# Four chained attention blocks on one core: the order of the first loads, of the first set-up instructions and of GpSimd's bias additions

## The chip, the cores and the metric

The kernel runs on one NeuronCore of a Trainium2 chip. The core has five engines that run side by side, each with an instruction queue of its own: TensorE (PE in the profile; PEld is its weight load), VectorE (DVE), ScalarE (ACT), GpSimd (POOL) and SyncE (SP). SP here only issues DMAs; ACT issues some too. 16 DMA engines carry the transfers of all queues. The metric is device microseconds (us) of one execution, and lower is better. Before the change it is 2193.79 us, the median of three runs (2191.36 to 2203.49).

## The reference

`x` is 8 batches x 256 tokens x 320 channels, all float32. Four layers follow each other, each working on the result of the one before:

```python
x = L0(x, ctx)   # self attention, cross attention, GEGLU; q, k, v and softmax weights rounded to 8 bits
x = L1(x, ctx)   # the same three steps without rounding
x = L2(x, ctx)   # two cross attentions (text and image tokens), sum, projection, residual
x = L3(x, ctx)   # cross attention with 8 heads plus a second attention over channels
```

The change touches L0 alone, whose two attentions are (20 heads of 16 channels):

```python
h = layer_norm(x);  q, k, v = fq(h @ Wq1), fq(h @ Wk1), fq(h @ Wv1)
x = softmax_q(q k^T / 4) v @ Wo1 + bo1 + x          # self
h = layer_norm(x);  q, k, v = fq(h @ Wq2), fq(ctx @ Wk2), fq(ctx @ Wv2)
x = softmax_q(q k^T / 4) v @ Wo2 + bo2 + x          # cross
```

`fq` divides by the largest magnitude in the whole tensor over 127, rounds, and multiplies back. `softmax_q` does the like with the softmax weights (over 255). So a step for all 8 batches has to end before any rounding can start.

## The kernel before

`x` stays in SBUF as `x_sb` (128 partitions, 16 token tiles, 320 channels). `Kernel.__init__` (L56) starts its load: `load_x` (L77) issues batch 0 on SP's queue and batches 1 to 7 on ACT's (L80). It then issues the loads of `cols` (gains, biases and small masks, one column each) on ACT's queue (L65, L67, L68; the second and third write rows that the first wrote too) and builds the identity matrices.

`open_flow` (L160) opens the pools and makes small masks on VectorE: `m32`, `half`, `magic` (L168 to L176). `open_quant` (L179) makes `place`, `rows`, `fill`, `sel` in the same manner (L184 to L202). None of these is needed by the first normalisation.

`load` (in `tile_xattn_kernel`, L1642) loads a layer's weights on SP's queue. `weight_q` (L233) is used for q and k of L0: 8 DMAs each, for each block of rows one of 256 channels (L242) and one of the last 64 channels, spread to 4 heads of 16 with gaps of 16 (L243, pieces of 64 bytes). `weight_v` (L263) makes 4 DMAs (L269), `weight_o` (L272) 5 (L276, L279), `load_ctx` (L82) 3 (L86).

The program is written with a scheduler that orders each engine's queue itself, from dependencies and its own estimates: what stands late in the text can be issued early. In the trace SP's queue has the 256-channel parts of q and k ahead of v, and the 64-byte parts of q and k only after a part of o and of ctx. GpSimd's bias additions, which stand late in the text (L1428), are issued soon after the last reader of their operand.

`Quant` (L1192) is one attention of L0; `s` is the self attention, `c` the cross one.

- `project_all` (L1218): for each batch, `normed` (L305) computes the mean and variance on VectorE (L314, L315, L317), the reciprocal root on GpSimd (L319), the normalised `xh` on VectorE (L322); `turned` (L327) transposes it on TensorE (L339) and ScalarE applies gain and bias (L347, four pieces, of which the last two take rows of `cols` in both halves); `duo`, `half_rows` and `whole_rows` (L122 to L139) multiply with v, q and k. The row blocks of 64 channels come first (L139), so that two of them run side by side on TensorE, and the next batch's transposes stand between them and the whole blocks (L132).
- `steps` (L1316) reduces the maxima to one scale each. `whole`, `whole_by_act`, `whole_v` (L1344, L1369, L1386) round q, k and v, mostly on GpSimd. `whole_all` (L1409) runs them all, and at its end adds the projection's bias row to `x`, one batch at a time, on GpSimd (L1428, 128 partitions x 640).
- `tops_all` (L1438) finds the row maxima (PE L1453, DVE L1456), splits them into three bf16 parts on VectorE (L1473, L1475), and `sums_all` (L1508) sums the exponentials (PE L1497 and L1519, ACT L1504). These two and `whole_all` are woven together.
- `weight_steps` (L1545) turns the sums into one scale (ACT L1549 and L1557, DVE L1552 to L1558); `shift` (L1561) makes each batch's offsets, nearly all on VectorE (L1565 to L1570).
- `out_all` (L1572) makes the weights (DVE L1606), multiplies with v (PE L1588), projects and adds to `x` (DVE L493), which needs the bias to be in it already. With the self attention's `out_all` run the cross attention's `queries_all` (L1288): `normed` again, with `xh` on GpSimd for six batches, and TensorE L120.

`behind` (L293) gives the scheduler an edge that puts one instruction after another on the same engine, without a semaphore. After L0 come L1 to L3 as a flow of `items`; the change does not touch them.

Of the kernel before, what the change touches and what calls it, by code (L numbers as in the profile page):

```python
# [11 lines left out]
F32 = mybir.dt.float32  # L12
BF16 = mybir.dt.bfloat16
AF = mybir.ActivationFunctionType
# [40 lines left out]
class Kernel:  # L55
    def __init__(self, ctx, tc, a, out):  # L56
        self.ctx, self.tc, self.nc, self.a, self.out = ctx, tc, tc.nc, a, out
        self.persist = ctx.enter_context(tc.tile_pool(name="persist", bufs=1))
        self.small = ctx.enter_context(tc.tile_pool(name="small", bufs=4))
        nc, pool = self.nc, self.persist  # L60

        self.x = pool.tile([P, NT, C], F32, name="x_sb")
        self.load_x(0, B)
        self.cols = pool.tile([P, NCOL], F32, name="cols_sb")
        nc.scalar.dma_start(self.cols, a["cols"])  # L65

        nc.scalar.dma_start(self.cols[64:, NCOL - H3 * T3 :], a["cols"][:64, NCOL - H3 * T3 :])  # L67
        nc.scalar.dma_start(self.cols[64:, 2:COL_B1:3], a["cols"][:64, 2:COL_B1:3])  # L68
        self.ident = pool.tile([P, P], F32, name="ident")
        make_identity(nc, self.ident)  # L70
        self.ident16 = pool.tile([P, P], BF16, name="ident16")
        nc.vector.tensor_copy(self.ident16, self.ident)
        self.nhalf = pool.tile([P, TPB], F32, name="nhalf")
        nc.gpsimd.memset(self.nhalf, -0.5)
        self.ctxT = pool.tile([P, 2, B, M], F32, name="ctxT")

    def load_x(self, b0, b1):  # L77
        xt = self.a["x"].rearrange("b (t p) c -> p (b t) c", p=P)
        for b in range(b0, b1):
            (self.nc.scalar if b else self.nc.sync).dma_start(self.x[:, TPB * b : TPB * (b + 1), :], xt[:, TPB * b : TPB * (b + 1), :])  # L80

# [78 lines left out]
    def open_flow(self, ctx):  # L160
        nc, tc = self.nc, self.tc
        self.ps_f = ctx.enter_context(tc.tile_pool(name="ps_f", bufs=3, space=PSUM))
# [3 lines left out]
        self.work = ctx.enter_context(tc.tile_pool(name="f_work", bufs=2))  # L166

        self.m32 = fk.tile([P, PAD], F32, name="m32")  # L168
        nc.vector.tensor_reduce(self.m32, self.ident.rearrange("p (j r) -> p r j", r=PAD), AX.X, ALU.add)
# [6 lines left out]
        nc.vector.tensor_scalar(self.magic[:, 2:4], self.half, -MAGIC, None, ALU.mult)  # L176
        self.count = 0

# [46 lines left out]
    def rows_of(self, w, src, filled=False):  # L225
# [5 lines left out]
        return [(w[:, 0], src[:P]), (w[:64, 1], src[P:])]  # L231

    def weight_q(self, tag, name, filled=False):  # L233


        n = -(-self.a[name].shape[0] // P)
        w = self.fw.tile([P, n, 3 * P], F32, tag=tag, name=tag)
        if n == 2 or filled:
            self.nc.gpsimd.memset(w[64:, 1] if n == 2 else w[:64, 2], 0.0)
        self.nc.gpsimd.memset(w[:, :, 2 * P :], 0.0)  # L240
        for dst, src in self.rows_of(w, self.a[name], filled):
            self.nc.sync.dma_start(dst[:, : 2 * P], src[:, : 2 * P])  # L242
            self.nc.sync.dma_start(  # L243
                dst[:, 2 * P :].rearrange("p (h r) -> p h r", r=PAD)[:, :, :D],
                src[:, 2 * P :].rearrange("p (h d) -> p h d", d=D),
            )
        return w
# [57 lines left out]
    def normed(self, b, ln, on=None):  # L305
# [15 lines left out]
        for t in range(TPB):  # L321
            (on or nc.vector).tensor_scalar(  # L322
                xh[:, t], x[:, t], mv[:, t, 0:1], rstd[:, t : t + 1], ALU.subtract, ALU.mult
            )
# [867 lines left out]
class Quant:  # L1192
# [25 lines left out]
    def project_all(self):  # L1218
# [8 lines left out]

        x = k.normed(0, self.ln)
        after = turn(0)
        for b in range(B):  # L1230
            xT = after
            if b + 1 < B:
                x = k.normed(b + 1, self.ln)
            q = self.q[b] = self.pool.tile([P, 3 * N], F32, tag="Q", name="Q", bufs=B)
# [151 lines left out]
    def whole_v(self, b):  # L1386
# [10 lines left out]
        for s in range(2):  # L1397
# [5 lines left out]
        yield  # L1403
        nc.gpsimd.tensor_scalar(
            vh[:ks, :kc, 16:, :D], tv[:ks, :kc, 2 * P :].rearrange("p t (h d) -> p t h d", d=D),
# [3 lines left out]
    def whole_all(self, b0=1):  # L1409
# [16 lines left out]
        for b in range(B):  # L1426
            x = k.x[:, TPB * b : TPB * (b + 1), :]
            k.nc.gpsimd.tensor_tensor(x, x, self.brow.unsqueeze(1).to_broadcast([P, TPB, C]), ALU.add)  # L1428
            yield
# [207 lines left out]
def kernel(ctx: ExitStack, tc: tile.TileContext, a, out):  # L1637
    k = Kernel(ctx, tc, a, out)
    with ExitStack() as es:
        k.open_flow(es)  # L1640

        def load(layer, q, kk, v, o, row):  # L1642
            plain = layer == "L0"
            w = {"q": k.weight_q("q", f"{layer}_xattn_{q}", q == "Wq2")}
            if kk is not None:
                w["k"] = (k.weight_q if plain else k.weight_k)("k", f"{layer}_xattn_{kk}")
                w["v"] = k.weight_v("v", f"{layer}_xattn_{v}")
            if o is not None:
# [6 lines left out]
        with tc.tile_pool(name="l0", bufs=1) as pool:  # L1655
            k.open_quant(pool)
            with tc.tile_pool(name="l0_keys", bufs=1, side="right") as kpool:
                s = Quant(k, pool, kpool, 0, *load("L0", "Wq1", "Wk1", "Wv1", "Wo1", 0), False)
                k.load_ctx()
                s.project_all()  # L1660
# [162 lines left out]
```

## Time and profile before

| what | value |
|---|---|
| runs | 2203.49, 2193.79, 2191.36 us |
| span of the profiled execution, first to last instruction | 2202.1 us |
| mean granted TensorE clock | 0.971 |
| TensorE busy | 2036.4 us, 92% |
| VectorE, ScalarE, GpSimd busy | 1112.6, 833.3, 330.5 us |
| first batch of `x` in SBUF (VectorE starts) | 4.51 us |
| ScalarE's table load | 15.90 us, 1.28 us long |
| last part of k's weights in SBUF (TensorE goes on) | 23.95 us |
| end of `project_all` on TensorE | 100.8 us |
| last instruction of `whole_v` on GpSimd, self / cross | 187.9 / 541.3 us |
| the 16 bias additions L1428 | first at 16.1, last at 396.2 us, 1.53 us shortest, 2.54 us longest |

The page of a profile gives the busy time of each engine, the busy tenths in 40 slices of the span, the chain of work that ended last, and groups of equal instructions with what ended the idle time before them. The trace can be asked further: the chain in order of time, the instructions of one engine in order of time (start, length, engine, line, operation, result<-operands, count), who waited for whom, and busy times by window. Only the span of the profiled execution is on the page; it lies 1.4 us under the slowest of the three runs.

### The profile page before, as it was taken

What the parts mean: (1) busy time and instruction counts of PE and PEld (TensorE: products, weight loads), DVE (VectorE), ACT (ScalarE), POOL (GpSimd) and SP (SyncE); (2) the same over time, 40 slices, a digit from 0 to 9 for tenths busy, and PEclk for the clock granted to TensorE, in tenths of its full rate; (3) what the DMA queues carried; (4) which work ended last, traced back from release to release, by engine and by line L of the source; (5) the groups of instructions that cost most, each with busy time, mean ns of one, the idle gap of its engine ahead of it and who ended that gap; (6) DMA issues with size and microseconds to landing.
All of it is one profiled execution on the core that took longest, in us unless ns stands there. A gap on an engine that the chain in (4) does not pass through costs nothing.

```text
span 2202.1 us, 38254 instructions
## 1 busy us (share of the span) xinstructions
PE 2036.4 (92%) x16415; PEld 1194.6 (54%) x16415; DVE 1112.6 (51%) x1698; ACT 833.3 (38%) x1259; POOL 330.5 (15%) x358
## 2 busy tenths in 40 slices
PE   7888889898889999999999998899999999999997
PEld 5643345554444465465555555544555655666664
DVE  5388687445651222235555567621121666546565
ACT  3456888367542121124444444311201333222221
POOL 3194033723010000000000010100000100000100
PEclk9989889898899999999999999999999999999999
DMA  4000000642120000020000101100000120000000
GB/s 118 20 12 2 2 1 1 174 111 57 52 85 14 1 0 1 1 93 2 2 2 22 28 25 36 47 1 0 1 0 1 24 68 23 19 16 26 23 19 16
DMA packets 79303, 63.21 MB, mean 29 GB/s; under 512 B 48410, under 2 KB 68318, under 8 KB 78622
## 3 DMA queue, kind: packets, MB, share of 16 engines
q1 hardware_dynamic: 75070, 57.06, 9.4%
q10 hardware_dynamic: 4064, 3.71, 0.6%
q8 instruction: 129, 2.11, 0.4%
q14 instruction: 40, 0.33, 0.0%
HBM read 42.61 MB, written 17.37 MB: 27 GB/s over the span
## 4 chain that ended last, share of the span: by engine, by line
PE 73%; DVE 15%; issue 4%; ACT 4%; POOL 2%; DMA 2%; SPq 0%; ACTq 0%; DVEq 0%; POOLq 0%
PE pf L594 13%; PE pf L120 11%; PE pf L132 9%; PE pa L120 7%; PE pa L456 6%; PE pf L439 4%; PE pa L594 3%; PE pf L139 3%; DVE negm L1456 3%; PE pf L394 3%; PE pf L736 3%; DVE rs L464 3%; PE pf L1497 2%; PE pa L1519 2%; DVE negm L401 2%
## 5 line engine op out<-in xcount | busy, mean ns | idle before, releaser
L445 ACT ACTIVATE e<-pf 128x1024 f32<-128x1024 f32 (+2 forms) x176 | 158.5, 946 | 220.1 <-PE pf L439 213.1
L401 DVE TENSOR_REDUCE negm<-pf 128x4 f32<-128x1024 f32 (+4 forms) x224 | 188.1, 887 | 97.9 <-PE pf L394 97.9
L594 PE MATMUL pf<-xTf,ff 128*128 128x512 f32 x512 | 230.8, 597 | 6.2 <-DVE negm L401 5.2
L464 DVE RECIPROCAL rs<-pa 128x256 f32<-128x256 f32 x88 | 152.3, 1745 | 143.5 <-PE pa L456 143.5
L1504 ACT ACTIVATE e<-pf,sc_s 128x1024 f32<-128x1024 f32 x160 | 169.8, 1118 | 48.7 <-PE pf L1497 44.8
L1456 DVE TENSOR_REDUCE negm<-pf 128x4 f32<-128x1024 f32 (+2 forms) x128 | 143.3, 1151 | 69.6 <-PE pf L1453 58.2
L619 DVE SCALAR_TENSOR_TENSOR hT<-pf,cols_sb,gl 128x512 f32<-128x512 f32 x64 | 48.0, 751 | 256.4 <-ACT gl L618 254.1
L120 PE MATMUL pf<-ff,hT 128*128 128x320 f32 x640 | 174.4, 434 | 0.0
L594 PEld LDWEIGHTS pf<-xTf,ff 128*128 128x128 f32 x512 | 94.3, 190 | 125.4 <-issue 118.5
L120 PEld LDWEIGHTS pf<-ff,hT 128*128 128x128 f32 x640 | 120.9, 190 | 55.5 <-issue 6.1
L618 ACT ACTIVATE gl<-pf,cols_sb 128x512 f32<-128x512 f32 x64 | 44.0, 689 | 247.8 <-PE pf L594 247.8
L439 PE MATMUL pf<-qT,kT 32*128 32x256 f32 (+1 forms) x1280 | 122.1, 410 | 9.1 <-DVE negm L401 7.5
L394 PE MATMUL pf<-kT,qT 32*128 32x120 f32 (+1 forms) x1920 | 113.1, 326 | 18.6 <-ACT e L445 18.3
L487 POOL TENSOR_TENSOR xb<-x_sb,brow 128x640 f32<-128x640 f32 x24 | 37.0, 1543 | 563.8 <-DVE x_sb L493 555.4
L120 PE MATMUL pa<-o,oT 128*128 128x320 f32 x352 | 105.7, 441 | 15.2 <-DVE oT L465 15.2
L394 PEld LDWEIGHTS pf<-kT,qT 32*128 32x128 f32 x1920 | 83.0, 186 | 58.4 <-ACT e L445 27.5
L647 POOL TENSOR_TENSOR xb<-x_sb,brow 128x640 f32<-128x640 f32 x16 | 25.0, 1563 | 573.8 <-DVE x_sb L652 528.2
L1497 PE MATMUL pf<-Q,K 32*128 32x256 bf16 (+1 forms) x960 | 90.5, 295 | 21.7 <-DVE negm L1456 11.5
L456 PE MATMUL pa<-e,v 128*32 128x256 f32 (+1 forms) x1280 | 106.1, 391 | 2.3 <-ACT e L445 1.7
L1606 DVE TENSOR_SCALAR w<-e 128x1024 bf16<-128x1024 f32 (+2 forms) x128 | 89.2, 703 | 32.3 <-ACT e L1504 31.1
L132 PE MATMUL pf<-xT,q 128*128 128x256 f32 x384 | 100.5, 391 | 0.4 <-ACT e L445 0.2
L439 PEld LDWEIGHTS pf<-qT,kT 32*128 32x128 f32 (+1 forms) x1280 | 68.4, 182 | 55.5 <-DVE negm L401 26.9
(291 smaller groups left out, 3439.2 us busy)
## 6 DMA issues: line engine op xcount, KB each, us to landing
ff<-in_L_xattn_Wff_dram SPq DMA_DIRECT2D x1, 2560.0 KB
qT<-nT SPq DMA_DIRECT2D x160, 4.0 KB
ff<-in_L_xattn_ff_w_dram SPq DMA_DIRECT2D x1, 2560.0 KB
out_dram<-x_sb SPq DMA_DIRECT2D x16, 160.0 KB
kd_cross<-kst SPq DMA_DIRECT2D x8, 300.0 KB
vd_cross<-vst SPq DMA_DIRECT2D x8, 300.0 KB
vd_both<-vst SPq DMA_DIRECT2D x8, 300.0 KB
kT<-kd_cross SPq DMA_DIRECT2D x8, 300.0 KB
```

The source lines that it names most:

```text
L120: self.nc.tensor.matmul(out, l, r, start=i == 0, stop=i == len(pairs) - 1)
L132: self.nc.tensor.matmul(o, *t[c], start=start and c == 0, stop=stop and c == n - 1, skip_group_check=True)
L394: nc.tensor.matmul(s[j // 2][:, j % 2, o : o + nk], qT[r : r + PAD, g, t * P : (t + 1) * P], kT[r : r + PAD, g, :nk], start=True, stop=True,)
L401: nc.vector.tensor_reduce(negm[:, n, 2 * i : 2 * i + 2, g0 : g0 + len(gs), :].rearrange("p j g t -> p j (g t)"), sv[:, :, :, k0:k1], AX.X, ...
L439: nc.tensor.matmul(s[j // 2][:ks, j % 2, o : o + N], kT[r : r + PAD, g, c * ks : (c + 1) * ks], qT[r : r + PAD, g, :], start=True, stop=True,)
L445: nc.scalar.activation(e[:ks, 2 * i : 2 * i + 2, :n], s[i][:ks, :, :n], AF.Exp, scale=scale)
L456: nc.tensor.matmul(o[j * PAD : (j + 1) * PAD, what * N : (what + 1) * N], w, es[g][:ks, j, c * N : (c + 1) * N], start=first and c == 0 an ...
L464: nc.vector.reciprocal(rs, o[:, N:])
L594: ins = nc.tensor.matmul(*args, **kw)
L1456: nc.vector.tensor_reduce(negm[:, 2 * h : 2 * h + 2, gs[0] : gs[-1] + 1, :].rearrange("p j g t -> p j (g t)"), s[:, :, : len(gs) * TPB * n ...
L1497: nc.tensor.matmul(s[at // 2][:ks, at % 2, o : o + N], l, m, start=not shift and o == 0, stop=shift and o + N == n, skip_group_check=True,)
L1504: nc.scalar.activation(e[:ks, :, :n], ps[:ks, :, :n], AF.Exp, scale=self.sc[:ks, 9:10])
```

## The change

First loads: batch 0 of `x` is issued at the start and all of `x` is on SP's queue. For L0's first weights SP's order is written out (the scheduler may not change SP's order there): x0, v, x1, q, x2, k, x3 to x7, o, ctx. ScalarE gets a small activation on `nhalf` that needs nothing loaded. The memsets of the padded columns of q and k come before the first normalisation. `self.first` is the normalisation of batch 0, made before the masks; the masks' VectorE instructions and each further normalisation's VectorE instructions of `project_all` are put behind the last `xh` of the normalisation before. The bias additions of both attentions are put behind the last instruction of `whole_v`'s last batch.

```diff
         self.x = pool.tile([P, NT, C], F32, name="x_sb")
-        self.load_x(0, B)
+        self.load_x(0, 1)
...
-        nc.vector.tensor_copy(self.ident16, self.ident)
         self.nhalf = pool.tile([P, TPB], F32, name="nhalf")
         nc.gpsimd.memset(self.nhalf, -0.5)
+        early = self.small.tile([P, TPB], F32, tag="early", name="early", bufs=1)
+        nc.scalar.activation(early, self.nhalf, AF.Identity)
...
-            (self.nc.scalar if b else self.nc.sync).dma_start(self.x[:, TPB * b : TPB * (b + 1), :], xt[:, TPB * b : TPB * (b + 1), :])
+            self.nc.sync.dma_start(self.x[:, TPB * b : TPB * (b + 1), :], xt[:, TPB * b : TPB * (b + 1), :])
...
+        self.blank = {n: self.blank_q(n, 3) for n in "qk"}
+        self.first = self.normed(0, 0)
+        with self.later():
+            self.open_masks(fk)
+        self.count = 0
+
+    def later(self):
+
+        return self.tc.issue_after(self.scaled.ins)
+
+    def open_masks(self, fk):
+        nc = self.nc
+        nc.vector.tensor_copy(self.ident16, self.ident)
...
+    def blank_q(self, tag, n):
+
+        w = self.fw.tile([P, n, 3 * P], F32, tag=tag, name=tag)
+        self.nc.gpsimd.memset(w[:, :, 2 * P :], 0.0)
+        return w
+
     def weight_q(self, tag, name, filled=False):
...
-        w = self.fw.tile([P, n, 3 * P], F32, tag=tag, name=tag)
+        w = self.blank.pop(tag, None) or self.blank_q(tag, n)
         if n == 2 or filled:
             self.nc.gpsimd.memset(w[64:, 1] if n == 2 else w[:64, 2], 0.0)
-        self.nc.gpsimd.memset(w[:, :, 2 * P :], 0.0)
...
-            (on or nc.vector).tensor_scalar(
+            self.scaled = (on or nc.vector).tensor_scalar(
...
-        x = k.normed(0, self.ln)
+        x = k.first
         after = turn(0)
         for b in range(B):
             xT = after
             if b + 1 < B:
-                x = k.normed(b + 1, self.ln)
+                with k.later():
+                    x = k.normed(b + 1, self.ln)
...
-        nc.gpsimd.tensor_scalar(
+        self.put = nc.gpsimd.tensor_scalar(
             vh[:ks, :kc, 16:, :D], tv[:ks, :kc, 2 * P :].rearrange("p t (h d) -> p t h d", d=D),
...
-            k.nc.gpsimd.tensor_tensor(x, x, self.brow.unsqueeze(1).to_broadcast([P, TPB, C]), ALU.add)
+            k.behind(
+                k.nc.gpsimd.tensor_tensor(x, x, self.brow.unsqueeze(1).to_broadcast([P, TPB, C]), ALU.add), self.put
+            )
             yield
...
-            w = {"q": k.weight_q("q", f"{layer}_xattn_{q}", q == "Wq2")}
+            w = {}
+            if q == "Wq1":
+                w["v"] = k.weight_v("v", f"{layer}_xattn_{v}")
+                k.load_x(1, 2)
+            w["q"] = k.weight_q("q", f"{layer}_xattn_{q}", q == "Wq2")
+            if q == "Wq1":
+                k.load_x(2, 3)
             if kk is not None:
                 w["k"] = (k.weight_q if plain else k.weight_k)("k", f"{layer}_xattn_{kk}")
-                w["v"] = k.weight_v("v", f"{layer}_xattn_{v}")
+                if q == "Wq1":
+                    k.load_x(3, B)
+                else:
+                    w["v"] = k.weight_v("v", f"{layer}_xattn_{v}")
...
-            k.open_quant(pool)
+            with k.later():
+                k.open_quant(pool)
             with tc.tile_pool(name="l0_keys", bufs=1, side="right") as kpool:
-                s = Quant(k, pool, kpool, 0, *load("L0", "Wq1", "Wk1", "Wv1", "Wo1", 0), False)
-                k.load_ctx()
+                with tc.manual_schedule(engines={mybir.EngineType.SP}):
+                    first = load("L0", "Wq1", "Wk1", "Wv1", "Wo1", 0)
+                    k.load_ctx()
+                s = Quant(k, pool, kpool, 0, *first, False)
```

`issue_after` adds such an edge, without a semaphore, to each instruction of its block that runs on the engine of the instruction given, here VectorE. The shape and the number of the additions, the masks and the loads stay as they were.

## The prediction

> **What bounds the kernel now.** I read the busy line of the page first, then the chain of waits in order of time for the first 120 us, then the single engines there, then GpSimd up to 600 us, since the change moves GpSimd's work that far.
>
> ```profile
> PE 2036.4 (92%) x16415; PEld 1194.6 (54%) x16415; DVE 1112.6 (51%) x1698; ACT 833.3 (38%) x1259; POOL 330.5 (15%) x358
> ```
>
> TensorE is the bound over the whole, so time is won only where TensorE stands still. The chain shows where that is at the start (columns: start, length, what):
>
> ```profile
> 9.19 4.81 DMA v<-in_L_xattn_Wv_dram
> ...
> 14.02 5.98 DMA ctxT<-in_ctxT_dram
> ...
> 20.07 0.37 SPq L243
> ...
> 21.69 2.12 DMA k<-in_L_xattn_Wk_dram
> 23.81 0.14 issue
> 23.95 0.67 PE pf L139 x2
> 24.61 0.81 PE pa L339 x6
> 25.42 7.34 PE pf L132 x32
> ...
> 95.84 4.96 PE pf L132 x22
> ```
>
> Until 23.95 the chain is loads: SP waits for landings of v and of ctx (not needed for another 100 us) before it can issue the 64-byte parts of q and k. From 23.95 to 100.80 it is TensorE alone, 10.17 us a batch. So whatever the start of that stretch gains, its end gains too, and `steps`, which needs all eight maxima, with it.
>
> Before that, the first batch itself is late:
>
> ```profile
> 11.98 1.54 DVE L200 CAST sel<-selc 128x640 bf16<-128x640 f32 x2
> 13.44 1.51 DVE L322 TENSOR_SCALAR xh<-x_sb,mv,rstd 128x320 f32<-128x320 f32 x4
> ```
> ```profile
> 14.59 0.60 ACTq L67 DMA_DIRECT2D cols_sb<-in_cols_dram  x1
> 15.22 0.65 ACTq L68 DMA_DIRECT2D cols_sb<-in_cols_dram  x1
> 15.90 1.28 ACT L347 ACT_TABLE_LOAD   x1 [15.90 <-DMA brow<-in_rows_dram]
> 17.20 1.47 ACT L347 ACTIVATE xT<-pa,cols_sb 128x256 f32<-128x256 f32 x3
> 20.61 0.56 ACT L347 ACTIVATE xT<-pa,cols_sb 64x256 f32<-64x256 f32 x1 [1.94 <-DMA cols_sb<-in_cols_dram]
> ```
>
> VectorE starts on x0 at 4.51, yet writes its first `xh` at 13.44, after the statistics of five other batches and the masks. ScalarE's table load and the late rows of `cols` follow.
>
> **The start, worked out.** Two paths meet at the last k product (23.95 now).
>
> *Loads.* In the new order 23 issues go up to k's last one: x0, 4 for v, x1, 8 for q, x2, 8 for k. The rows give 0.54 us an issue for q's large parts (4 in 2.17) and 0.56 for k's small ones (4 in 2.23); I take 0.55. The last is issued at 0.73 + 22 x 0.55 = 12.8 and lands 2.12 later, as now: 14.9. Bytes do not decide: 2400 KB at the 271 GB/s of the first 20 us are 9.1 us. Bounds: with the shortest issue on SP (0.33) 10.1; with the longest (0.65) and a landing as slow as v's 4.81, 19.8.
>
> [...]
>
> *First batch.* If x0 lands at 4.0 (4.51 now beside other loads; 2.85 if as fast as k's last piece), VectorE's rows give statistics 0.89, aggregates 0.24, 0.15 for `ve`, GpSimd's `rstd` 0.69, two `xh` 0.89: 6.9. The transposes start at the first `xh` (6.5) and take 1.68; the first piece of `xT` 0.56 after it: 8.8. The v products take 3.4 (17.82 to 21.2 now), the rest up to k's last 2.1 (21.55 to 23.65 now): 14.3. Bounds by x0's landing: 13.2 and 14.8.
>
> The table load (1.28) is hidden behind x0's flight, if ScalarE's three issues for `cols` do not hold it up; they need `cols`' first part landed, so it ends by about 7 us (0.74 + two landings of 2.12 + 1.25 + 1.28), still ahead of 8.2. The masks (10.50 to 13.44 now) run after `xh` of batch 0 and before batch 1, 9.9, and batch 1's 2.9 us end at 12.8, before its transposes at 15.6: free. If that cover went, 2.9 us. What is queued behind: all of batch 1 to 7's statistics, which TensorE wants at 10 us a batch.
>
> [...]
>
> The later path decides: 14.9 against 23.95, **-9.0 us**; bounds -10.8 and -4.1. Late next: k's small parts, then TensorE itself, 0.6 us behind.
>
> **The additions.** Sixteen instructions of 1.53 us, 24.5 us, change their place. What one does to VectorE shows here (first GpSimd, then VectorE):
>
> ```profile
> 16.05 3.11 POOL L1428 TENSOR_TENSOR x_sb<-x_sb,brow 128x640 f32<-128x640 f32 x2 [5.16 <-DMA brow<-in_rows_dram]
> ```
> ```profile
> 15.73 2.04 DVE L322 TENSOR_SCALAR xh<-x_sb,mv,rstd 128x320 f32<-128x320 f32 x2
> 17.69 1.50 DVE L317 TENSOR_SCALAR ve<-mv 128x2 f32<-128x2 f32 x1
> 19.10 0.48 DVE L314 BATCH_NORM_STATS2 bnst<-x_sb 128x6 f32<-128x320 f32 x1
> ```
>
> `ve`, 0.16 us elsewhere, ends with the addition. In the trace all TENSOR_SCALARs on SBUF wait like this, and a scalar_tensor_tensor under L647 (1.39 instead of 0.48); statistics and reads of PSUM (L401, L1598) do not.
>
> *Self attention, first eight.* Now beside the projection, where TensorE has the end: leaving gains 0. They go behind 187.9 (the last L1404), into 102.74 us in which GpSimd is idle, beside `tops_all`. VectorE there mostly reduces from PSUM, but five small instructions a batch work on SBUF:
>
> ```profile
> L1473 DVE CAST npx<-negm 128x40 bf16<-128x40 f32 x12 | 12.7, 1059 | 0.2
> ```
> ```profile
> L1473 DVE CAST npx<-negm 128x40 bf16<-128x40 f32 x9 | 1.7, 191 | 0.2
> ```
>
> The first is 110 to 185 us, with GpSimd busy; the second 200 to 245, with it idle. 12.3 us of additions meet one such burst (196.8 now): 3 x 0.87 + 2 x 0.09 = 2.8, of which I take 1.5, as the sums' products can go ahead. Bounds 0 and 5 x 1.53 = 7.7.
>
> *Cross attention, second eight.* They leave 292 to 398 us. There seven L1606 under an addition take 1.50 instead of 0.69: 5.7 us of VectorE. But TensorE is 91% busy there and waits for ScalarE (L347), so I take -0.5; bounds 0 and -5.7. They go behind this row:
>
> ```profile
> 540.98 0.36 POOL L1404 TENSOR_SCALAR V<-tv 120x64 bf16<-120x64 f32 x1
> 572.43 1.54 POOL L647 TENSOR_TENSOR xb<-x_sb,brow 128x640 f32<-128x640 f32 x1 [31.09 <-DVE x_sb L493]
> ```
>
> GpSimd is idle there for 31.09 us, but 541.4 to 553.7 is just `weight_steps` and the first `shift`: VectorE is busy for 4.79 and 4.97 of 5 us from 545 and from 550, nearly all on SBUF, and TensorE waits for it (2.63 of 5 from 545). Queued behind: L1606, L1588, L493. Bounds: 0, if every addition slips into a gap of VectorE, and 12.3, if VectorE stands for all eight; a gain is excluded, as nothing leaves there. Nearest row: the seven L1606 lost 5.7 of 13.0 us (7 x 1.86). That share of 12.3 is 5.4; VectorE has slack again from 560 (3.0 of 5), so I take **+4.0**.
>
> **Sum**: -9.0 + 1.5 - 0.5 + 4.0 = -4.0. It is made against the span of 2202.1 (2198.1), which lies by the slowest of the three runs; I carry the difference to the median: 2193.8 - 4.0 = **2189.8 us**.
>
> **Rivals.** (All against 2193.8; 0.5%, about what a measurement of this kernel tells from no change, is 11 us: 2182.8 and 2204.8.)
> 1. *The additions vanish in idle time.* For it: GpSimd's idle 102 and 31 us. Against: the waits above. With half of the 5.7 us of L1606 coming back: -9.0 - 2.9 = -11.9, 2182; with the start's best (-10.8) 2180.
> 2. *The additions take over: slower.* VectorE's serial chain from L503 to L1570 (542.1 to 546.7) has nine SBUF instructions; if each lets one addition pass, all eight stand in it, 8 to 12 us, and the self attention's burst costs up to 7.7. It decides once both together pass the start's 9.0: -9.0 + 12.3 + 2.8 = +6, 2200; at all upper ends +11, 2205. Against: back-to-back instructions of VectorE got ahead of a waiting addition at 292.5 (it took 2.54).
> 3. *The start does not come early.* SP waits for landings now (2.9 us for x0 alone). If k ends at 19.8, -4.1 + 5.0 = +1: 2195.
>
> TensorE's granted clock is 0.63 and 0.50 in the five-us windows from 545 and 550; another length of that stall can move such windows by 2 or 3 us either way, whichever case holds.
>
> **How the numbers follow.** Forecast 0.52 (its own range 2184 to 2196), rival 1 0.24, rival 2 0.12, rival 3 0.12. Faster by over 0.5% are three quarters of rival 1: 0.18. Slower by over 0.5% are half of rival 2: 0.06. Within: 0.76. The range, 2180 to 2201, leaves out the far ends of rivals 1 and 2.
>
> **What would show it.** Right: the last product with k's 64 rows at 14 to 16 us, TensorE without a gap from there, `steps` 9 us earlier; L1428 sixteen times behind the last L1404s; longer L1473 around 190 and longer L1565 to L1570 in `weight_steps`, with `out_all` of the cross attention less early than the 9 us. Wrong: k's last part after 18; additions beside short VectorE instructions; a new wait for x1 or `cols` in the first batches.

## The result and the profile after

| | median us | runs | ratio to before, 95% interval |
|---|---|---|---|
| before | 2196.74 | 4 (2191.36 to 2203.49) | |
| changed kernel | 2269.93 | 4 (2262.05 to 2271.17) | 1.0306 [1.0276, 1.0336] |

The change makes the kernel 3% slower; the prediction was 2189.8, with a range up to 2201. The profiled execution took 2271.17 us, its span 2269.4: 67.3 more than the 2202.1 of before. Behind the new functions the changed kernel's lines lie up to 21 further down: L1428 is L1448, L1504 is L1525, L1456 is L1477, L1473 is L1494, L1565 is L1586, L339 is L357, L132 is L133.

TensorE is busy for 12.8 us more than before (2036.4 us), at a mean granted clock of 0.952 instead of 0.971; the other 54.5 of the 67.3 us are idle time. The page's busy line, and one line of its groups (busy, mean ns of one, then the idle time of the engine ahead of the group and what ended most of it):

```profile
PE 2049.2 (90%) x16415; PEld 1202.3 (53%) x16415; DVE 1100.5 (48%) x1698; ACT 831.4 (37%) x1260; POOL 326.8 (14%) x358
...
L1525 ACT ACTIVATE e<-pf,sc_s 128x1024 f32<-128x1024 f32 x160 | 169.3, 1116 | 93.4 <-POOL x_sb L1448 50.1
```

The second line names the culprits as a pair that ought not to know each other: the exponentials of `sums_all`, on ScalarE, waited 50.1 us for a bias addition on GpSimd. They do not read `x_sb`. The busy times of the stretch from 150 to 200 us (stretch, its length, then TensorE, its weight load, VectorE, ScalarE, GpSimd, granted clock, DMA share, GB/s) show how far it reached; before, then after:

```profile
150.00:200.00 50.00, 41.32 (x594) 16.79 (x589) 40.50 (x47) 33.65 (x35) 37.96 (x58) 0.89 0.01 2
```
```profile
150.00:200.00 50.00, 2.89 (x32) 1.17 (x31) 1.84 (x3) 2.79 (x4) 45.48 (x63) 0.52 0.02 3
```

TensorE, VectorE and ScalarE stand together; only GpSimd works. What ScalarE stood at is seen in its own instructions in order of time, where an issue of a DMA is a line too (ACTq), and in GpSimd's beside them:

```profile
143.69 2.12 ACT L1525 ACTIVATE e<-pf,sc_s 128x1024 f32<-128x1024 f32 x2 [1.61 <-PE pf L1518]
195.51 0.33 ACTq L115 DMA_DIRECT2D brow<-in_rows_dram  x1
195.95 2.12 ACT L1525 ACTIVATE e<-pf,sc_s 128x1024 f32<-128x1024 f32 x2 [50.14 <-POOL x_sb L1448]
```
```profile
183.54 11.94 POOL L1448 TENSOR_TENSOR x_sb<-x_sb,brow 128x640 f32<-128x640 f32 x8
```

The additions end at 195.48, the issue goes out at 195.51, the exponentials go on at 195.95. The issue belongs to `bias_row` (L115): it loads one of the kernel's eight bias rows into a tile `brow`, of which there are three buffers, and it does so **on ScalarE's queue**. The fourth row goes into the buffer of the first, the row that the self attention's eight additions read. So it has to wait for the last of them, and with it, in order, all that ScalarE has queued behind. The fifth row takes the buffer of the second and waits for the cross attention's additions (577.42 to 589.37):

```profile
571.25 0.47 ACT L1545 ACTIVATE sums<-pa,fill 128x256 f32<-128x256 f32 x1
589.40 0.33 ACTq L115 DMA_DIRECT2D brow<-in_rows_dram  x1
589.83 3.27 ACT L1525 ACTIVATE e<-pf,sc_c 120x1024 f32<-120x1024 f32 x4 [18.11 <-POOL x_sb L1448]
```

The same two issues were in the trace of before, with the same wait, where it cost nothing. ScalarE, then GpSimd:

```profile
66.00 2.06 ACT L347 ACTIVATE xT<-pa,cols_sb 128x256 f32<-128x256 f32 x4 [1.21 <-PE pa L339]
68.67 0.34 ACTq L114 DMA_DIRECT2D brow<-in_rows_dram  x1
70.91 0.59 ACT L1257 COPY Q<-pf 128x512 f32<-128x512 f32 x1 [2.85 <-PE pf L132]
```
```profile
67.10 1.54 POOL L1428 TENSOR_TENSOR x_sb<-x_sb,brow 128x640 f32<-128x640 f32 x1 [8.64 <-DVE xh L322]
```

The last self addition ended at 68.64 and the row's load went out at 68.67, in a gap of ScalarE that ends with TensorE. After the change the scheduler has put the two issues back in ScalarE's order as well, by its own estimates, but only behind the instructions that end at 145.8 and 571.7: 50 and 18 us too early.

The start, on TensorE after the change; before, the second batch's transposes stood at 24.54:

```profile
8.05 1.68 PE L357 MATMUL pa<-ident,xh 128*128 128x128 f32 x6 [8.05 <-DVE xh L340]
9.96 3.42 PE L133 MATMUL pf<-v,xT 128*128 128x320 f32 x8 [0.23 <-ACT xT L365]
...
16.36 0.70 PE L140 MATMUL pf<-xT,k 64*128 64x256 f32 x2 [1.81 <-DMA k<-in_L_xattn_Wk_dram]
...
18.61 1.36 PE L357 MATMUL pa<-ident,xh 128*128 128x128 f32 x6
19.77 3.13 PE L133 MATMUL pf<-xT,q 128*128 128x256 f32 x8
22.73 1.89 PE L133 MATMUL pf<-xT,k 128*128 128x256 f32 x8
```

The transposes are 5.9 us earlier, the end of `project_all` only 4.3 (96.55 against 100.80): eight products that take 1.89 us at 22.73 took 3.13 at 19.77.

**The account:** stalls 50.1 + 18.1 = 68.2, start -4.3, together 63.9 of the 67.3. The sum fits better than its parts. At the self attention's first scaled output (L1598 at 277.99 before, L1619 at 316.15 after) the changed kernel is 38.2 us behind, and not 50.1 - 4.3 = 45.8. At the cross attention's first sum into `x` (L493 at 566.89, L511 at 621.39) it is 54.5 behind, and the rest comes later. These gains and losses of up to 8 us behind the stalls I have not traced.

### The profile page after: what moved, and what is told of

Same layout as the page of the kernel before. It is cut to its first block, busy times and chain, and to the rows that moved or that the text cites. A ratio compares the mean times of both kernels' runs of the same rounds, so it can differ in the third digit from the quotient of the medians.

```text
span 2269.4 us, 38249 instructions
## 1 busy us (share of the span) xinstructions
PE 2049.2 (90%) x16415; PEld 1202.3 (53%) x16415; DVE 1100.5 (48%) x1698; ACT 831.4 (37%) x1260; POOL 326.8 (14%) x358
## 3 DMA queue, kind: packets, MB, share of 16 engines
q8 instruction: 129, 2.11, 0.4%
## 4 chain that ended last, share of the span: by engine, by line
PE 70%; DVE 12%; POOL 7%; issue 5%; ACT 4%; DMA 2%; SPq 0%; ACTq 0%; DVEq 0%; POOLq 0%
PE pf L612 13%; PE pf L121 10%; PE pf L133 9%; PE pa L121 7%; PE pa L474 6%; PE pf L457 4%; PE pa L612 3%; PE pf L140 3%; PE pf L412 3%; PE pf L754 3%; DVE rs L482 2%; PE pf L1518 2%; DVE negm L419 2%; DVE negm L1477 2%; DVE rs L1147 2%
## 5 line engine op out<-in xcount | busy, mean ns | idle before, releaser
L1525 ACT ACTIVATE e<-pf,sc_s 128x1024 f32<-128x1024 f32 x160 | 169.3, 1116 | 93.4 <-POOL x_sb L1448 50.1
L1477 DVE TENSOR_REDUCE negm<-pf 128x4 f32<-128x1024 f32 (+2 forms) x128 | 143.4, 1133 | 115.0 <-PE pf L1474 108.5
L1525 ACT ACTIVATE e<-pf,sc_c 120x1024 f32<-120x1024 f32 (+1 forms) x96 | 88.3, 979 | 48.6 <-PE pf L1518 28.7
L1474 PE MATMUL pf<-K,Q 32*128 32x256 bf16 (+1 forms) x640 | 50.1, 261 | 60.7 <-ACT e L1525 49.8
L133 PE MATMUL pf<-xT,q 128*128 128x256 f32 x384 | 102.7, 397 | 0.4 <-ACT e L463 0.2
```

The source lines that it names most:

```text
L133: self.nc.tensor.matmul(o, *t[c], start=start and c == 0, stop=stop and c == n - 1, skip_group_check=True)
L1477: nc.vector.tensor_reduce(negm[:, 2 * h : 2 * h + 2, gs[0] : gs[-1] + 1, :].rearrange("p j g t -> p j (g t)"), s[:, :, : len(gs) * TPB * n ...
L1525: nc.scalar.activation(e[:ks, :, :n], ps[:ks, :, :n], AF.Exp, scale=self.sc[:ks, 9:10])
```

## The experiments

Theory S: ScalarE's queue stands at the load of a bias row whose buffer the late additions still read. Rivals: the late additions hold VectorE (L), or the changed start costs something later (V). Times are medians; each ratio is to the kernel before, run on the same chip.

### The start alone

```diff
-            k.behind(
-                k.nc.gpsimd.tensor_tensor(x, x, self.brow.unsqueeze(1).to_broadcast([P, TPB, C]), ALU.add), self.put
-            )
+            k.nc.gpsimd.tensor_tensor(x, x, self.brow.unsqueeze(1).to_broadcast([P, TPB, C]), ALU.add)
```

> The changed kernel with its bias additions left where they were before (no dependence on `whole_v`); order of the loads, early activation and set-up behind the first norm stay. Theory S (ScalarE stands behind the load of a bias row that must wait for the additions): the two stalls of 50.1 and 18.2 us are gone, and what is left is what the start gained on TensorE, 4.3 us at the end of the projection: 0.998 of before, about 2192 us, end of the projection on TensorE at 96 to 97 us. Rival V (the changed start itself, by its contention or clock, cost something later on): 1.005 or more. By the prediction's sum of the start alone, -9.0 us: 0.996.

Measured: 2196.01 us, 0.9969 [0.9947, 0.9992]. The slowness is gone with the late additions alone, so rival V falls. The gain, 0.31% or 6.8 us, has 1.8 to 11.7 in its interval and does not tell 4.3 from 9.0.

### The additions alone

```diff
-        nc.gpsimd.tensor_scalar(
+        self.put = nc.gpsimd.tensor_scalar(
...
-            k.nc.gpsimd.tensor_tensor(x, x, self.brow.unsqueeze(1).to_broadcast([P, TPB, C]), ALU.add)
+            k.behind(
+                k.nc.gpsimd.tensor_tensor(x, x, self.brow.unsqueeze(1).to_broadcast([P, TPB, C]), ALU.add), self.put
+            )
```

> The kernel before with the bias additions alone moved behind the last instruction of `whole_v`; loads, table load and set-up as before. Theory S: the load of the fourth bias row comes ahead of the attention's exponentials in ScalarE's order and waits for the last addition; ScalarE stands about 50 us near 145 to 195 and about 18 us near 570 to 590: +68 us, 1.031, 2265 to 2275 us. Rival L (the additions hold VectorE, as the prediction feared): +5 to +15 us, at most 1.007, and no idle stretch of ScalarE over 5 us that ends with a load's issue. If the changed start is needed for the stall (the rows' loads come that early only with it): within 0.5% of before.

Measured: 2267.63 us, 1.0288 [1.0242, 1.0335]. ScalarE waits for an addition twice, 50.6 and 19.2 us. The changed start is not needed for it.

### The self attention's additions alone

```diff
-                k.nc.gpsimd.tensor_tensor(x, x, self.brow.unsqueeze(1).to_broadcast([P, TPB, C]), ALU.add), self.put
+                k.nc.gpsimd.tensor_tensor(x, x, self.brow.unsqueeze(1).to_broadcast([P, TPB, C]), ALU.add),
+                None if self.cross else self.put,
```

> The changed kernel with the cross attention's eight additions left where they were before; the self attention's eight stay behind `whole_v`. Theory S: the stall that ends with the self's last addition, 50.1 us, stays, and the one near 577 to 590 goes: 50 less the start's 4.3 us gives 1.020 to 1.024 of before, about 2245 us. If only one of the two stalls could cost anything (the other one's work finds slack further on): 1.000 or 1.031.

Measured: 2248.16 us, 1.0211 [1.0168, 1.0255]; one wait of ScalarE for an addition, 50.4 us. In this run's profile the projection ends 5.7 us early; 50.4 - 5.7 = 44.7, and 2.11% are 46.5 (37 to 56 by the interval). The changed kernel's 67 us are 21 more, near the second stall's 18.1: the two stalls add up.

### The first layer's rows in buffers of their own

This is the test of theory S that keeps the additions where the change puts them and only takes away the reason to wait:

```diff
-        t = pool.tile([P, C], F32, tag="brow", name="brow", bufs=3)
+        t = pool.tile([P, C], F32, tag="brow0" if i < 2 else "brow", name="brow", bufs=2)
```

> The changed kernel, its additions still moved, but the bias rows of the first layer's two attentions lie in two buffers of their own, and the later rows in two others, so that no early load of a row has to wait for an addition. Theory S: both stalls go; left are the start's -4.3 us and what 16 additions beside VectorE's bursts cost, 0 to +6 us: 0.998 to 1.001, 2190 to 2200 us. Rival L (VectorE, or x itself, is held by the late additions): the time stays within 5 us of the changed kernel's, 1.028 to 1.031.

Measured: 2218.46 us, 1.0073 [1.0045, 1.0101]. Nobody waits for an addition any more, and 51 of the 67 us are back. But 2190 to 2200 was expected: 22 us are missing against the start alone. Rival L, which explained nothing in the changed kernel, stands behind the stall. VectorE, then GpSimd:

```profile
190.36 7.73 DVE L1494 CAST npx<-negm 128x40 bf16<-128x40 f32 x1
198.13 0.20 DVE L1496 TENSOR_TENSOR negm<-negm,npx 128x40 f32<-128x40 f32 x1
198.36 0.20 DVE L1494 CAST npx<-negm 128x40 bf16<-128x40 f32 x1
...
545.33 0.15 DVE L1577 TENSOR_SCALAR sc_c<-most 128x1 f32<-128x1 f32 x1
545.52 0.21 DVE L1579 TENSOR_SCALAR sc_c<-sc_c 128x1 f32<-128x1 f32 x1
545.87 11.50 DVE L1586 TENSOR_SCALAR rem<-sums,sc_c 128x256 f32<-128x256 f32 x2
```
```profile
186.02 12.03 POOL L1448 TENSOR_TENSOR x_sb<-x_sb,brow 128x640 f32<-128x640 f32 x8
...
544.95 11.95 POOL L1448 TENSOR_TENSOR x_sb<-x_sb,brow 128x640 f32<-128x640 f32 x8
```

A cast of 0.20 us took 7.73 and ended with the last of the eight additions (198.05). Of two shifts, 0.41 each where GpSimd is idle, the first stood from 545.87 until the run of additions was over. That is 7.5 + 10.7 = 18.2 us, with TensorE waiting (8.16 and 12.1 us) each time; the other 4 of the 22 us are open. Each addition is 1.5 us long: these two instructions were not let in between them. Not all of VectorE's work stands: L1577 and L1579, one number for each partition, took 0.15 and 0.21 us beside the first addition.

### Four buffers for the rows

```diff
-        t = pool.tile([P, C], F32, tag="brow", name="brow", bufs=3)
+        t = pool.tile([P, C], F32, tag="brow", name="brow", bufs=4)
```

> The changed kernel with four buffers for the bias rows instead of three. The fourth row's load then has a free buffer and waits for nobody; the fifth, which comes early in ScalarE's order as well, has to wait for the self attention's last addition. Theory S: the first stall of about 50 us stays (another row's load makes it), the second, near 577 to 590, goes, and where it stood VectorE meets the run of eight additions without cover, +11 us as with the rows in buffers of their own: -4 + 50 + 11 = +57 us, 1.024 to 1.027, about 2255 us. If one more buffer frees ScalarE altogether: 1.007, as with buffers of their own.

Measured: 2265.06 us, 1.0296 [1.0259, 1.0332]. The first half of the expectation holds, the second does not: both stalls are there.

```profile
198.10 0.33 ACTq L115 DMA_DIRECT2D brow<-in_rows_dram  x1
198.53 2.12 ACT L1525 ACTIVATE e<-pf,sc_s 128x1024 f32<-128x1024 f32 x2 [50.17 <-POOL x_sb L1448]
```
```profile
592.29 0.33 ACTq L115 DMA_DIRECT2D brow<-in_rows_dram  x1
592.73 3.28 ACT L1525 ACTIVATE e<-pf,sc_c 120x1024 f32<-120x1024 f32 x4 [19.15 <-POOL x_sb L1448]
```

With one more buffer the fifth and the sixth row take the places of the fourth and the fifth. The scheduler issues a row as early as its buffer allows, so another buffer only changes which row waits.

### The rows issued by GpSimd

```diff
-        self.nc.scalar.dma_start(t, self.a["rows"][i : i + 1, :].to_broadcast([P, C]))
+        self.nc.gpsimd.dma_start(t, self.a["rows"][i : i + 1, :].to_broadcast([P, C]))
```

> The changed kernel, three buffers as before, but the bias rows' loads are issued by GpSimd, the engine that runs the additions: in its order a row's load that reuses a buffer stands behind the additions anyway. Theory S: no load waits on ScalarE's queue, both stalls go, and the time is that of the kernel with buffers of their own, 1.005 to 1.010 (2213 to 2223 us). If what costs is the lateness of x or of the rows and not ScalarE's place in the wait: 1.025 to 1.031, as the changed kernel.

Measured: 2210.74 us, 1.0044 [1.0022, 1.0066], just under the first expectation and far from the second. Both stalls are gone. Three buffers are enough if the load stands on the queue of the engine that reads the row. The burst of the self attention happened to fall behind its run of additions; the cross attention's run cost 10 us, at a copy of 128 numbers in one partition:

```profile
538.86 10.05 DVE L521 COPY row<-top 1x128 f32<-1x128 f32 x1
```

### Pauses between the additions

On top of buffers of their own, each addition also waits for an exponential:

```diff
+            sync = mybir.DependencyInfo(mybir.DependencyClass.Sync, mybir.DependencyReason.DATA)
+            k.tc.add_manual_dep(add.ins, k.pace.ins.name, sync, reason="pace")
...
-            nc.scalar.activation(e[:ks, :, :n], ps[:ks, :, :n], AF.Exp, scale=self.sc[:ks, 9:10])
+            k.pace = nc.scalar.activation(e[:ks, :, :n], ps[:ks, :, :n], AF.Exp, scale=self.sc[:ks, 9:10])
...
-            k.weave((0, c.out_all()), (0, k.paced(rest(), 1)))
+            k.weave((0, c.out_all()), (1, c.adds()), (0, k.paced(rest(), 1)))
```

> As with the first layer's rows in buffers of their own, but each of the 16 additions also waits for an exponential of ScalarE a little earlier in the program (the self's eight one by one among the last exponentials of `sums_all`, the cross attention's eight among those of `out_all`), so that GpSimd pauses between two additions. Without this, VectorE's first small SBUF instruction met all that was left of a run of eight additions: a cast of 0.20 us took 7.73, two shifts of 0.41 took 11.50. Theory R (a waiting VectorE instruction is let in only where GpSimd pauses, so a run of additions counts as one): a hold is at most one addition, 1.5 us, and some 18 us come back: 0.997 to 1.001, about 2197 us. Theory A (each VectorE instruction pays for the additions that it meets one by one, and the run's length does not matter): 1.005 to 1.010, as without the pauses.

Measured: 2205.03 us, 1.0018 [1.0001, 1.0035], between the two expectations. Of the 22 us, 12 came back. The additions also stand later now, at 214 to 232 and at 547 to 580 us, so the time alone does not tell pauses from places; the single rows do. No hold is longer than one addition, even where five stand without a visible pause (VectorE, GpSimd, ScalarE):

```profile
217.30 0.21 DVE L1501 CAST npx<-negm 128x40 bf16<-128x40 f32 x1
217.54 1.48 DVE L1503 TENSOR_TENSOR negm<-negm,npx 128x40 f32<-128x40 f32 x1
219.06 1.45 DVE L1501 CAST npx<-negm 128x40 bf16<-128x40 f32 x1
220.55 1.46 DVE L1503 TENSOR_TENSOR negm<-negm,npx 128x40 f32<-128x40 f32 x1
```
```profile
214.42 7.53 POOL L1453 TENSOR_TENSOR x_sb<-x_sb,brow 128x640 f32<-128x640 f32 x5 [28.81 <-ACT e L1532]
```
```profile
218.87 1.11 ACT L1532 ACTIVATE e<-pf,sc_s 128x1024 f32<-128x1024 f32 x1 [0.70 <-PE pf L1525]
```

But now each VectorE instruction of a burst pays, three times 1.3 us here; and VectorE's instructions get in between two additions. Theory R is not quite it, since GpSimd's row shows no pause. If exponentials and additions are paired in order, the fifth addition waits for the exponential that ends at 219.98. That is 0.4 us before its own start (220.40), but after the fourth had started (218.91): it was released only while the one ahead of it ran.

### Waits that were met long before

Is it the wait as such that opens the way, or that the addition really has to wait? Buffers of their own again, additions where the change puts them, each waiting for one of the attention's first eight exponentials (`self.done[b]` instead of `k.pace`).

> The additions where the change puts them, the first layer's rows in buffers of their own, and each addition with a wait of its own that was met long before (one of the attention's first eight exponentials). With the pauses of the paced version VectorE was let in after each addition (a cast of 0.21 us ran in the middle of a run that shows no gap); without them it stood 7.73 and 11.50 us. Theory Q (only an addition that really has to wait opens the way): the cast near 190 and the two shifts near 546 stand as long as without waits, 6 to 8 and 10 to 12 us. Theory W (any wait in the instruction opens the way): no VectorE instruction stands over 2 us.

Measured once: 2218.62 us, and the holds of the version without waits, to 0.01 us:

```profile
187.14 7.72 DVE L1495 CAST npx<-negm 128x40 bf16<-128x40 f32 x1
...
542.66 11.50 DVE L1588 TENSOR_SCALAR rem<-sums,sc_c 128x256 f32<-128x256 f32 x2
```

A wait that was met long before changes nothing, as theory Q says. Its other half, that an addition has to stand and wait, is more than the paced run shows: there it was enough that the release came while the addition ahead was running.

### The start, taken apart

*The loads alone*: the changed start without the early activation, `self.first` and `later()`:

```diff
-        early = self.small.tile([P, TPB], F32, tag="early", name="early", bufs=1)
-        nc.scalar.activation(early, self.nhalf, AF.Identity)
...
-        self.blank = {n: self.blank_q(n, 3) for n in "qk"}
-        self.first = self.normed(0, 0)
-        with self.later():
-            self.open_masks(fk)
+        self.blank = {}
+        self.open_masks(fk)
```

> Of the changed start, the order of the loads alone: no early activation, no norm ahead of the masks, VectorE's order free, additions as before. The prediction's two paths: the loads let k's last product come at 17.5 as in the changed kernel, but the first batch stays late (first transposes near 13.9, ScalarE's table load behind its own loads), so the first v product comes at 17 to 18 and the second batch's transposes at 22 to 24.5 instead of 18 to 19 in the changed kernel and 24.5 before. If the loads were all of it: 18 to 19.

*All but the loads*: `load` and `load_x` as before, SP's order free, the rest of the changed start kept:

```diff
-        self.load_x(0, 1)
+        self.load_x(0, B)
...
-                with tc.manual_schedule(engines={mybir.EngineType.SP}):
-                    first = load("L0", "Wq1", "Wk1", "Wv1", "Wo1", 0)
-                    k.load_ctx()
+                first = load("L0", "Wq1", "Wk1", "Wv1", "Wo1", 0)
+                k.load_ctx()
```

> Of the changed start, all but the loads: early activation, first norm ahead of the masks, masks and further norms behind it; loads and additions as before. By the prediction the loads then decide alone: first transposes near 8, but k's last product at 24 as before, the second batch's transposes at 24 to 25 and the end of the projection at 100 to 101: nothing gained. If the first batch was the bound: 20 or less.

Measured once each (TensorE's second batch of transposes, before at 24.54; loads alone, then all but the loads):

```profile
22.14 0.87 PE L353 MATMUL pa<-ident,xh 128*128 128x128 f32 x6
```
```profile
24.11 0.87 PE L357 MATMUL pa<-ident,xh 128*128 128x128 f32 x6
```

Loads alone gain 2.4 us, set-up alone 0.4, both together 5.9: neither half is enough. But both halves are held by the first batch, and by no load of weights. With the loads alone its transposes start at 14.48. With the set-up alone they start at 8.32, but the first v product is at 17.16, because ScalarE issues seven loads of `x` first and `cols` only at 10.95:

```profile
17.16 4.64 PE L133 MATMUL pf<-v,xT 128*128 128x320 f32 x8 [7.16 <-ACT xT L365]
...
13.10 2.83 SPq L261 DMA_DIRECT2D k<-in_L_xattn_Wk_dram  x4
```

The second line shows that the loads did not stay as before either: SP, ordered by the scheduler again, issues k's small parts from 13.10 instead of 20.07, and TensorE waits for none of them. So the 24.11 agrees with "24 to 25" by chance, and this run does not test the path of the loads. What shows that path are TensorE's own waits for k: 0.29 us before, 1.81 and 0.49 after the change.

*Rows behind k, batches 1 and 2 of `x` behind k* (additions where they were):

```diff
-        self.nc.scalar.dma_start(t, self.a["rows"][i : i + 1, :].to_broadcast([P, C]))
+        (self.nc.sync if i < 2 else self.nc.scalar).dma_start(t, self.a["rows"][i : i + 1, :].to_broadcast([P, C]))
...
-                k.load_x(1, 2)
...
-            if q == "Wq1":
-                k.load_x(2, 3)
...
-                    k.load_x(3, B)
+                    k.load_x(1, B)
```

> The changed start with the additions where they were, and three more edits on the loads: batches 1 and 2 of `x` come behind k instead of between v, q and k, and the first two bias rows are issued by SyncE behind the output weights instead of early by ScalarE. Theory F (SyncE stood still because eight loads were in flight, 0.9 us for x0's landing and 2.0 for v's, besides two issues for x1 and x2): k's last product comes 2 to 4 us earlier than the 17.55 of the changed kernel, at 13.5 to 15.5, TensorE has hardly an idle stretch before it and its clock stays up; the projection ends at 92 to 95 instead of 96.6, 0.995 to 0.998 of before. If the landings themselves set the pace: the last k product at 17 to 18, and 0.997.

Measured: 2199.58 us, 0.9992 [0.9969, 1.0014]; a miss. k is early as expected (last product at 15.16 to 15.75), but batch 1 of `x` is now late (VectorE starts on it at 16.92), TensorE waits for its `xh`, and the projection ends only 2.0 us earlier. The transposes gain 4.9; the clock stands at half for 6.9 us between 17.4 and 27.6 (0.70, 0.50 and 0.79 in three windows of 3.4 us), which takes most of the difference:

```profile
15.16 0.59 PE L140 MATMUL pf<-xT,k 64*128 64x256 f32 x2
19.63 1.59 PE L357 MATMUL pa<-ident,xh 128*128 128x128 f32 x6 [3.88 <-DVE xh L340]
```

*Rows issued by GpSimd, batch 2 behind k, batch 1 ahead of q, additions where they were:*

```diff
-        self.nc.scalar.dma_start(t, self.a["rows"][i : i + 1, :].to_broadcast([P, C]))
+        self.nc.gpsimd.dma_start(t, self.a["rows"][i : i + 1, :].to_broadcast([P, C]))
...
-            if q == "Wq1":
-                k.load_x(2, 3)
...
-                    k.load_x(3, B)
+                    k.load_x(2, B)
```

> The changed start with the additions where they were, the bias rows' loads issued by GpSimd, and batch 2 of `x` issued behind k. In the run with the rows on GpSimd (and batch 2 ahead of k) the second batch's transposes came at 18.03 and the projection ended 6.5 us earlier than before, with no half-clock stretch. Theory F (fewer loads ahead of k on the shared eight in flight, less idle time of TensorE ahead of it): transposes at 17.0 to 17.8, no half-clock stretch in the first 40 us, projection 6.5 to 7.5 us earlier: 0.996 to 0.998 of before. If the clock falls all the same: 3 to 5 us earlier, 0.998 to 0.999.

Measured: **2192.14 us, 0.9960 [0.9945, 0.9975]**, faster than both kernels. The projection ends 7.3 us earlier than before, at the full clock (1.00 in every window from 12.0 to 27.6 us):

```profile
17.20 0.87 PE L357 MATMUL pa<-ident,xh 128*128 128x128 f32 x6
17.91 1.89 PE L133 MATMUL pf<-xT,q 128*128 128x256 f32 x8
```

## Why the prediction was wrong, step by step

- **"What is queued behind" the moved additions: the step that failed.** For the cross attention the prediction named the weights on VectorE (L1606), the products that read them (L1588) and the sum into `x` (L493); for the self attention only VectorE's burst. It asked who reads what an addition *writes*, and which of VectorE's instructions run beside it. It did not ask who next writes what an addition *reads*: the bias row's buffer, whose next writer is a DMA on ScalarE's queue. The rows at 68.64 and 68.67 of before show that link. The wait was there and free; moving its releaser by 127 us (68.6 to 195.5) made it 50.1 us. The self attention's additions alone give +46.5 us, both +67, and with the link cut +16. No rival had this wait in it.
- **The self additions, +1.5** (bounds 0 and 7.7). In the changed kernel VectorE stands anyway, and nothing shows. With ScalarE free the first cast lost 7.5, near the upper bound, and that is luck: the bound took a hold of one addition for each of five VectorE instructions; in fact the first one stood through the rest of the run and the others through nothing.
- **The cross additions, +4.0** (bounds 0 and 12.3). With ScalarE free 10.7, or 9.8 in the run with the rows on GpSimd. The nearest row, seven L1606 that lost 0.81 us on average, had single additions with pauses between them; a run of eight is another thing. Rival 2 had the right mechanism (VectorE stands in a serial chain) and a total of +6 to +11 against the median; the run with rows of their own lies at +16 (1.0073 of 2193.8, 10 to 22 by its interval). The start, which gives 4.7 us less than was taken there, would make up the rest of the way from +11.
- **Leaving 292 to 398 us, -0.5.** Right: with rows of their own the distance to before changes by 0.1 us from 302 to 383.
- **The start, -9.0** (bounds -10.8 and -4.1): mis-sized, 4.3. The path was right: after the change k is what TensorE waits for. Two terms were off. First, an issue took 0.55 to 0.57 us, as taken, but SP also stood: 0.8 us ahead of x1, 1.9 ahead of q, each time for an older load to land. The sum put such stands at nothing, though before had them and rival 3 names them. (It reads 2.9 us "for x0 alone"; the view has three waits of at most 1.2 us for loads of `x`.) The program signals these loads on eight semaphores in turn, so that x1's load (issued at 4.28) waits for the semaphore of x0's (issued at 0.73), and ScalarE's loads of `cols` and of the rows take turns among SP's. k's last issue was at 15.75 instead of 12.8. SyncE, after:

```profile
4.28 0.38 SPq L81 DMA_DIRECT2D x_sb<-in_x_dram  x1
6.58 0.33 SPq L260 DMA_DIRECT2D q<-in_L_xattn_Wq_dram  x1
```

  With the rows issued by GpSimd and all else as changed, q's first issue is at 4.64, but k's last only at 15.07; with batch 2 behind k as well they are at 4.40 and 13.98. Second, TensorE stood 1.8 us before k, with another gap of 0.5 behind it, and then ran at half clock from 18.8 for 3.4 us, which gives back 1.7: the granted clock is 0.71 in 17.4 to 20.8 us and 0.79 in the 3.4 us behind, that is 2.0 and 1.4 us at half (0.50 from 18.85 to 22.25). Less the stands (2.7) and this (1.7), 9.0 becomes 4.6, against 4.3 measured. The clock is the column behind the five engines, after the change and in the last run above:

```profile
17.40:20.80 3.40, 3.25 (x15) 2.54 (x16) 1.76 (x4) 1.22 (x3) 0.00 (x0) 0.71 0.93 257
```
```profile
17.40:20.80 3.40, 3.40 (x20) 3.06 (x19) 1.93 (x6) 2.02 (x4) 0.69 (x1) 1.00 0.99 289
```

  The run with the self attention's additions alone, with this same start and gaps of 1.64 and 0.41 us, had no half-clock stretch there and ended the projection 5.7 us early. With rows of their own (gap of 1.91) there was a stretch of 6.8 us, and the projection was 1.9 early; in the paced run (gap of 1.36) again 6.8 us, and 2.3 early; with waits met long before (gaps of 1.21 and 0.33) none, and 5.2 early. So with gaps of 1.2 to 1.9 us the half clock cost nothing or up to 3.4 us more, and their length does not decide it. That the gaps bring the half clock on is inferred from where it stands; no run shows it.
- **Free as predicted:** the table load (1.28 us as before, 1.21 to 2.49, the next activation at 2.50; wholly in x0's flight; the prediction's terms for its end add up to 7.5, where it says about 7) and the masks (8.27 to 11.3, behind batch 0's `xh`).

## What to carry to other kernels

Before an instruction is moved to a later time, follow its inputs as well as its output: whose buffer does it keep from being refilled, and on which engine's queue does that refill stand? A DMA issue that waits in a computing engine's queue can hold the engine: ScalarE stood 50.1 and 18.1 us behind two of them here. Put the reload on the queue of the engine that reads the buffer (2210.74 us here, against 2269.93), or give the buffer to nobody else (2218.46); one more buffer may only change which load waits (2265.06).

Small instructions bunched into one run on GpSimd are not the same as the same number spread out: what VectorE can lose is the rest of the run (7.5 and 10.7 of 12 us here), at whichever small step stands first, and that step may head a serial chain.

## What the runs showed of the hardware that was not expected

- Three VectorE instructions that met a run of GpSimd additions standing ready were let in only after the last: 7.73 us for a cast of 0.20, 11.50 for two shifts of 0.41, 10.05 for a copy of 128 numbers in one partition (0.21). With waits met long before: 7.72 and 11.50. Where each addition was released by ScalarE only while the one ahead of it ran, even with no gap in GpSimd's row, VectorE got in after each, and no instruction took over 1.8 us. What hands over in one case and not in the other is open.
- The prediction's reading that all TENSOR_SCALARs on SBUF wait for an addition is too wide: two of one number for each partition took 0.15 and 0.21 us beside one.
- With a half-clock stretch of 3.4 us behind gaps of 1.81 and 0.49 us the start gained 4.3 us, without one behind gaps of 1.64 and 0.41 it gained 5.7.
